# Loading the first batch ahead of the weights, and what shares memory with the set-up

## The chip, the cores and the metric

One core of one Trainium2 chip. The metric is the device time of one execution of the whole kernel in microseconds, the median over several runs. The profile is one further execution under the hardware profiler; it gives a span, from the first to the last instruction, and every instruction's place in it.

## The reference

32 graphs (batches b) of 512 nodes with 256 features. Two layers; each adds a graph attention and then a sequence model to x:

```python
# layer 0
x = x + gnn0(layernorm(x), adj, W, a_src, a_dst, ...)   # 4 heads, masked softmax over neighbours
x = x + mamba2(layernorm(x), W_in, conv_w, ..., W_lin)  # 512 channels, chunked scan over the nodes
# layer 1
x = x + gnn1(layernorm(x), adj, W, a)                   # one head
x = x + lstm(layernorm(x), W_ih, W_hh, ...)             # over the 512 nodes, with prefix and suffix sums
```

All in float32; adj is int32, 1 MB for each graph, and x 0.5 MB for each graph.

## The kernel before

The kernel runs two phases. `layers_per_batch` does layer 0 and the attention of layer 1 for each batch and writes the result to a buffer `X3` in device memory. `recurrence` then runs the LSTM of all 32 batches together, node by node. Between the two, a flag `odd` is read, and if it is set a general version of the first phase runs; with these inputs it isn't set.

**The set-up.** `layers_per_batch` first loads some 22 weights through the SP queue (`load_k` L96 for matrices, `load_row` L101 for rows spread over all partitions), in the order in which the code names them. Weights that only the set-up reads (`w0t`, `asrc`, `adst`, `normw`, `woutt`, `wlin`, `w1t`, `a1`) lie in a pool `wset`. From them TensorE (PE) makes the score weights of layer 0 (`pwa` L154, put into `sw0` by VectorE (DVE) at L205), of layer 1 (`pwb` L166, into `sw1` at L212) and the product `wc` of the output weights (`pwc` L243, L247). Then `wset` is closed, and the pools `io` (x and adj), `one`, `two` are opened over the same memory, so that a tile in them can be written only when the readers of what lay there are done.

**The batches.** `plain0(b)` loads adj (L474) and x (L476), normalises x (`layernorm` L65 to L71; its reciprocal root is two operations on GpSimd (POOL), `ve` L54 and `rs` L56), makes the mask and counts it (`msk` L481, `sqa` L483), turns x (`pxT` L262, `xT` L265), multiplies with `sw0` (`pra` L428), sends a row `linea` to device memory (L435) and has it spread over the partitions (`rb` L448), turns the mask (`pm` L493), projects (`phn` L507) and forms the weighted sum (`w` L461 and L467, `pav` L533). `after0` normalises the heads and adds to x (L319 to L337, POOL among them: L336, L337). `mamba_in` and `mamba_dt` prepare, `mamba` does the scan: `zs` L680, products of channels with decays read back through `ce` (L658) and `bc` (L736), POOL multiplications at L729, L776 and L800, and the output product `po` L830. `plain1` and `after1` do layer 1's attention and store to `X3`.

**The order.** Each part is a generator that yields between steps. `streams` holds one generator for each kind of work with a due time for each step, counted in batches; the step with the lowest due time is issued next:

```python
streams = [
    each((0.0, 1.0, mamba, 0)),
    each((-0.097, -0.026, mamba_in, 0), (-0.026, 0.192, mamba_dt, 0)),
    each((0.571, 0.86, second, -1), (0.86, 1.54, first, 2)),
    each((1.65, 1.76, after0, 2)),
]
```

From this order and its own costs of instructions a planner fixes at build time the order of every engine and of the SP queue; an instruction that is ready by its costs may come ahead of one that was issued earlier. On the chip each engine and queue follows its order and waits on semaphores.

**The recurrence's weights.** `recurrence_weights` (called rw here) is one more stream: it loads small pieces of the LSTM's weights (`rwl` L1061, `rwraw` L1097 and L1101), scales and reorders them on POOL (`ordered`: `rwt` L1050, L1054, L1105) and stores them to a buffer `wr` (L1089, L1109), which `recurrence` reads. Its due times run from 3.25 to about 25 batches. The first piece is issued while the streams are started, ahead of everything else.

Of the kernel before, what the change touches and what calls it, by code (L numbers as in the profile page):

```python
# [9 lines left out]
F32 = mybir.dt.float32  # L10
I32 = mybir.dt.int32
# [64 lines left out]
def layers_per_batch(ctx, tc, c, a, X3, odd=None, wr=None):  # L76
# [6 lines left out]
    nc = tc.nc  # L83
    nb = a.x.shape[0]
# [9 lines left out]
    def load_k(src, cols, name, pool=None):  # L94
        t = (pool or wp).tile([P, src.shape[0] // P, cols], F32, name=name)
        nc.sync.dma_start(out=t, in_=src.rearrange("(k p) c -> p k c", p=P))  # L96
        return t

    def load_row(src, name):
        t = wp.tile([P, src.shape[1]], F32, name=name)  # L100
        nc.sync.dma_start(out=t, in_=src.to_broadcast([P, src.shape[1]]))  # L101
        return t


    tri = wp.tile([P, P], F32, name="tri")
    late = wp.tile([P, P], F32, name="late")
# [14 lines left out]

    setup = ExitStack()
    wset = setup.enter_context(tc.tile_pool(name="wset", bufs=1))
    w0 = load_k(a.w0, D, "w0")
    w0t = load_k(a.w0t, D, "w0t", wset)
    asrc = load_k(a.asrc, T0, "asrc", wset)
    adst = load_k(a.adst, T0, "adst", wset)
    bias0 = load_row(a.bias0, "bias0")
    gamma = load_row(a.gamma, "gamma")
    beta = load_row(a.beta, "beta")  # L130
    win = load_k(a.win, DIN, "win")
    convw = load_k(a.convw, 4, "convw")
    convb = load_k(a.convb, 1, "convb")
    dtb = wp.tile([NH, 1], F32, name="dtb")
    nc.sync.dma_start(out=dtb, in_=a.dtb.rearrange("o h -> h o"))
    alog = load_row(a.alog, "alog")
    dcol = load_k(a.dcol, 1, "dcol")
    normw = load_k(a.normw, 1, "normw", wset)
    woutt = load_k(a.woutt, DI, "woutt", wset)
    wlin = load_k(a.wlin, D, "wlin", wset)  # L140
    blin = load_row(a.blin, "blin")
    w1 = load_k(a.w1, D, "w1")
    w1t = load_k(a.w1t, D, "w1t", wset)
    a1 = load_k(a.a1, 2, "a1", wset)

    def score_weights0(vec, half, name):

# [99 lines left out]
        nc.vector.tensor_scalar(wc[:, cc, :], pw[:, :D], normw[:, cc, :], None, ALU.mult)  # L247

    setup.close()
    io = ctx.enter_context(tc.tile_pool(name="io", bufs=2))  # L250
    one = ctx.enter_context(tc.tile_pool(name="one", bufs=1))
    two = ctx.enter_context(tc.tile_pool(name="two", bufs=2))

# [86 lines left out]
    def attention0(b, state):  # L340


        adj = io.tile([P, NT, N], I32, tag="adj", bufs=1, name=f"adj{b}")
        nc.sync.dma_start(out=adj, in_=a.adj[b].rearrange("(i p) j -> p i j", p=P))
        x = io.tile([P, NT, D], F32, tag="x", bufs=4, name=f"x{b}")
        nc.sync.dma_start(out=x, in_=a.x[b].rearrange("(i p) d -> p i d", p=P))
        xn = two.tile([P, NT, D], F32, tag="rowa", name=f"xn{b}")
        layernorm(nc, small, c, xn, x, NT)
        nc.gpsimd.tensor_tensor(x, x, beta.unsqueeze(1).to_broadcast([P, NT, D]), ALU.add)
# [120 lines left out]
    def plain0(b, state):  # L470


        adj = io.tile([P, NT, N], I32, tag="adj", bufs=1, name=f"adj{b}")
        nc.sync.dma_start(out=adj, in_=a.adj[b].rearrange("(i p) j -> p i j", p=P))  # L474
        x = io.tile([P, NT, D], F32, tag="x", bufs=4, name=f"x{b}")
        nc.sync.dma_start(out=x, in_=a.x[b].rearrange("(i p) d -> p i d", p=P))  # L476
        xn = two.tile([P, NT, D], F32, tag="rowa", name=f"xn{b}")
        layernorm(nc, small, c, xn, x, NT)
        nc.gpsimd.tensor_tensor(x, x, beta.unsqueeze(1).to_broadcast([P, NT, D]), ALU.add)
# [43 lines left out]
        for q in range(2):  # L523
# [3 lines left out]
            for m in range(NT // 2):  # L527
                w = weighted(rb, cols, 2 * q, m, adjT, f"{b}_{q}")
                yield
                for t in range(2):  # L530
                    j = 2 * m + t
# [5 lines left out]
                for t in range(2):  # L537
                    j = 2 * m + t
# [54 lines left out]
    def mamba_dt(b, state):  # L593

        mT = state["mT"]

        csr = one.tile([P, N], F32, tag="csr", name=f"csr{b}")
        dtr = csr[64 : 64 + NH, :]
        pd = bank(f"pdt{b}")
        for k in range(DK):  # L600
# [12 lines left out]
        raw = columns(dtr, c.ident[64 : 64 + NH, 64 : 64 + NH], f"raw{b}")  # L613
# [12 lines left out]
        q = small.tile([P, NT, NH], F32, tag="q", name=f"q{b}")  # L626
# [26 lines left out]
        nc.scalar.activation(dec.rearrange("p a i h -> p (a i h)"), pdc[:, : 2 * NT * NH], AF.Exp)  # L653
        yield

        ce = one.tile([P, NC, N - P], F32, tag="ce", name=f"ce{b}")
        for k in range(2):
            nc.sync.dma_start(  # L658
                out=ce[k * DS : (k + 1) * DS],
# [5 lines left out]
    def mamba(b, state):  # L665
        x, mT = state["x"], state["mT"]
# [16 lines left out]
        bT = one.tile([DS, N], F32, tag="bT", name=f"bT{b}")  # L683
        cT = one.tile([P, N], F32, tag="cT", name=f"cT{b}")
# [153 lines left out]
        ssr = one.tile([P, N], F32, tag="ssr", name=f"ssr{b}")  # L838
        nc.scalar.copy(ssr, pss)
        pst = bank(f"psc{b}")  # L840
        for i in range(NT):
# [121 lines left out]
    states = [{} for _ in range(nb)]  # L963
# [29 lines left out]
    ]  # L993
    if odd is not None:
        rw = ctx.enter_context(tc.tile_pool(name="rw0", bufs=1))
        streams.append(3.25 + (nb - 8) / 64 * n for n, _ in enumerate(recurrence_weights(nc, rw, a, wr)))
    END = nb + 10
    at = [next(t) for t in streams]
    while min(at) < END:
# [27 lines left out]
        nc.vector.tensor_scalar(odd, pf[:1, :1], P - 0.5, None, ALU.is_lt)  # L1027


def recurrence_weights(nc, pool, a, wr):  # L1030

# [13 lines left out]
    def tile_(p, n, tag):  # L1045
        return pool.tile([p, n], F32, tag=tag, name=tag)

    def ordered(raw, n, s):
# [5 lines left out]
            nc.gpsimd.tensor_scalar(halves[:, :, to, :], src, half[g] * s, None, ALU.mult)  # L1054
        return t


    wl = tile_(P, 2 * DK, "rwl")
    for q in range(Q):
        for l in range(2):  # L1060
            nc.sync.dma_start(  # L1061
# [2 lines left out]
            )  # L1064
    yield
    nc.gpsimd.tensor_tensor(wl[:, :DK], wl[:, DK:], wl[:, :DK], ALU.subtract)
    bl = tile_(P, 2, "rbl")
    nc.sync.dma_start(out=bl, in_=a.bl.to_broadcast([P, 2]))
    b = [tile_(P, 4 * J, f"rwraw{n}") for n in range(2)]
    for t, src in zip(b, (a.bih, a.bhh)):  # L1070
        nc.sync.dma_start(out=t[:Q], in_=src.rearrange("o (q r) -> (o q) r", q=Q))
    yield
# [7 lines left out]
    nc.sync.dma_start(out=wr[0][:, n0 + 2 * J : n0 + 2 * J + 8], in_=wr[1].rearrange("o (u p) -> p (o u)", p=P))  # L1080
    yield
    for n, src in enumerate((a.fw, a.bw)):
        t = tile_(P, W, "rwt")
        for q in range(Q):
            nc.sync.dma_start(out=t[q * GB : (q + 1) * GB, :J], in_=src[q : q + 1, :].to_broadcast([GB, J]))
        yield
        nc.gpsimd.tensor_scalar(t[:, :J], t[:, :J], 0.5, None, ALU.mult)
        yield
        nc.sync.dma_start(out=wr[0][:, n0 + n * J : n0 + (n + 1) * J], in_=t[:, :J])  # L1089
        yield  # L1090
    for n, (src, s) in enumerate(((a.wih, 1.0), (a.whh, 0.5))):
        for k in range(DK):
            for q in range(Q):
                raw = tile_(P, 4 * J, f"rwraw{q % 2}")
                cols = slice(q * 4 * J, (q + 1) * 4 * J)
                if n == 0:
                    nc.sync.dma_start(out=raw, in_=src[k * P : (k + 1) * P, cols])  # L1097
                else:
                    for r in range(Q):
                        r0 = r * J + k * 32  # L1100
                        nc.sync.dma_start(out=raw[r * 32 : (r + 1) * 32], in_=src[r0 : r0 + 32, cols])  # L1101
                yield
                t = ordered(raw, P, s)
                if n == 1:
                    nc.gpsimd.tensor_scalar(t[:, 4 * J : 4 * J + 1], wl[:, k : k + 1], 0.5, None, ALU.mult)  # L1105
                yield
                w = (4 * J, W)[n]
                o0 = n * nx + (k * Q + q) * w
                nc.sync.dma_start(out=wr[0][:, o0 : o0 + w], in_=t[:, :w])  # L1109
                yield  # L1110
# [361 lines left out]
```

## Time and profile before

| what | us |
|---|---|
| median of 3 runs (lowest, highest) | 4805.4 (4803.51, 4810.24) |
| the profiled execution | 4803.97 |
| its span | 4802.2 |
| busy in the span: PE / PE weight loads / DVE | 4177.1 / 2586.4 / 3438.4 |
| busy in the span: ScalarE (ACT) / POOL | 3084.4 / 1308.3 |
| first adj load leaves; last set-up product `wc` | 30.01; 29.50 |
| first `zs` of batch 0, 1, 31 | 129.1, 227.1, 3259.7 |
| first instruction of `recurrence` on DVE | 3369.95 |

In lines of the profile the columns are: start and duration in us, engine (SPq and ACTq are the queues that issue DMAs), source line, operation, tile written <- tiles read, shape, count, and in brackets the idle time of the engine just before, with what ended it. In a table by windows each engine's busy time stands with its number of instructions, then the granted PE clock as a share of full speed, the share of time in which the DMA engines were busy, and GB/s.

### The profile page before, as it was taken

How to read it: one execution, taken by the hardware profiler on the slowest of the kernel's cores; microseconds unless marked ns; L12 is line 12 of the kernel's file. 1: busy time of each engine (PE TensorE's matmuls, PEld its weight loads, DVE VectorE, ACT ScalarE, POOL GpSimd, SP SyncE). 2: the span in 40 equal slices, each digit the busy share in tenths (PEclk: the TensorE clock that was granted, in tenths of full speed). 3: DMA queues.
4: the chain of work that ended last, by engine and by line, in shares of the span. 5: the costliest groups of instructions: out<-in, count | busy, mean ns of one | idle time of the engine just before them, and what ended most of it. 6: DMA issues, size and time to landing. Idle time of an engine off the chain costs nothing. (4 is left out here: it accounts for less than half of the span.)

```text
span 4802.2 us, 105289 instructions
## 1 busy us (share of the span) xinstructions
PE 4177.1 (87%) x40654; PEld 2586.4 (54%) x40654; DVE 3438.4 (72%) x10207; ACT 3084.4 (64%) x6724; POOL 1308.3 (27%) x1012
## 2 busy tenths in 40 slices
PE   4888888888888888888888888887899999999993
PEld 2444454444444444444445444444677777777772
DVE  3566666677666666666666667664688888888887
ACT  3677667776777767677766777765455555555552
POOL 4333343333433334333334333341000000000000
PEclk7999999999999999999999999998999999999997
DMA  4221112211122111222112221111211111111115
GB/s 110 65 67 59 56 67 67 69 58 60 62 71 69 58 60 56 68 69 67 58 56 65 68 69 58 60 40 38 56 38 43 41 41 39 39 42 38 42 38 160
DMA packets 273672, 286.96 MB, mean 60 GB/s; under 512 B 152844, under 2 KB 224488, under 8 KB 270984
## 3 DMA queue, kind: packets, MB, share of 16 engines
q1 hardware_dynamic: 269784, 270.26, 19.1%
q10 hardware_dynamic: 3216, 9.81, 0.7%
q8 instruction: 324, 5.31, 0.5%
q14 instruction: 188, 1.54, 0.1%
q0 software_dynamic: 160, 0.04, 0.0%
HBM read 226.04 MB, written 37.11 MB: 55 GB/s over the span
## 5 line engine op out<-in xcount | busy, mean ns | idle before, releaser
L1263 PE MATMUL pg<-wall,h 128*32 128x128 f32 x16352 | 559.1, 276 | 13.6 <-DVE h L1340 10.3
L1240 PE MATMUL pu<-xTr,wall 128*128 128x256 f32 x2048 | 565.3, 399 | 0.0
L1263 PEld LDWEIGHTS pg<-wall,h 128*32 128x32 f32 x16352 | 419.2, 109 | 210.1 <-DVE h L1340 170.1
L467 DVE SCALAR_TENSOR_TENSOR w<-w,adjT 128x1024 f32<-128x1024 f32 x256 | 348.0, 1380 | 245.6 <-ACT w L461 245.6
L1323 ACT ACTIVATE z<-pg 128x128 f32<-128x128 f32 x1024 | 255.8, 278 | 249.6 <-PE pg L1263 248.6
L743 ACT ACTIVATE g<-bc,cs 128x128 f32<-128x128 f32 x1024 | 321.9, 391 | 137.8 <-PE py L811 137.8
L1240 PEld LDWEIGHTS pu<-xTr,wall 128*128 128x128 f32 x2048 | 348.7, 190 | 104.0 <-issue 76.4
L693 DVE SCALAR_TENSOR_TENSOR acc<-px,convw,acc 128x511 f32<-128x511 f32 (+2 forms) x480 | 347.2, 745 | 76.7 <-ACT acc L688 68.6
L1332 ACT ACTIVATE tc<-z 128x32 f32<-128x32 f32 x1024 | 234.4, 229 | 250.6 <-DVE z L1328 181.7
L461 ACT ACTIVATE w<-rb,neg,colsa 128x512 f32<-128x512 f32 x512 | 387.4, 806 | 11.8 <-DMA rb<-linea 7.4
L533 PE MATMUL pav<-w,hb 128*64 128x512 f32 x1024 | 351.2, 612 | 22.8 <-DVE w L467 22.8
L830 PE MATMUL po<-wc,xh 128*128 128x256 f32 x1024 | 283.5, 422 | 100.3 <-POOL xh L800 100.3
L729 POOL TENSOR_TENSOR ce<-ce,cT 128x384 f32<-128x384 f32 x128 | 185.2, 1477 | 665.2 <-ACT cT L701 648.0
L54 POOL TENSOR_SCALAR ve<-mv 128x4 f32<-128x4 f32 x32 | 6.2, 195 | 1292.0 <-DVE mv L1165 1292.0
L945 PE MATMUL pov<-wb,wv 128*128 128x257 f32 x1024 | 243.2, 390 | 90.8 <-DVE wv L467 90.8
L1252 PE MATMUL pg<-turner,xu 128*32 128x128 f32 (+1 forms) x8192 | 321.5, 273 | 0.0
L672 PE MATMUL px<-mT,win 128*128 128x512 f32 x640 | 306.8, 610 | 0.0
L1241 ACT ACTIVATE xu<-pu,wall 128x256 f32<-128x256 f32 x512 | 243.2, 475 | 89.1 <-PE pu L1240 74.8
L1327 DVE SCALAR_TENSOR_TENSOR ab<-z 128x64 f32<-128x64 f32 x1024 | 226.4, 221 | 83.0 <-ACT z L1323 57.0
L830 PEld LDWEIGHTS po<-wc,xh 128*128 128x128 f32 x1024 | 203.2, 213 | 145.5 <-POOL xh L800 116.2
L945 PEld LDWEIGHTS pov<-wb,wv 128*128 128x128 f32 x1024 | 191.4, 192 | 134.8 <-DVE wv L467 105.7
L56 POOL TENSOR_TENSOR rs<-ve,mhalf 128x4 f32<-128x4 f32 (+1 forms) x192 | 255.2, 1329 | 15.9
(244 smaller groups left out, 8865.6 us busy)
## 6 DMA issues: line engine op xcount, KB each, us to landing
bc<-line SPq DMA_DIRECT2D x128, 512.0 KB
adj<-in_adj_dram SPq DMA_DIRECT2D x32, 1024.0 KB
rb<-linea SPq DMA_DIRECT2D x64, 512.0 KB
ce<-line SPq DMA_DIRECT2D x64, 384.0 KB
x<-in_x_dram SPq DMA_DIRECT2D x32, 512.0 KB
X<-x SPq DMA_DIRECT2D x32, 512.0 KB
xt<-X SPq DMA_DIRECT2D x128, 128.0 KB
x<-X SPq DMA_DIRECT2D x128, 128.0 KB
```

Of the source, the lines that this page charges most:

```text
L461: nc.scalar.activation(w[:, t, k, :], rb[:, k, :], AF.Relu, bias=neg1, scale=cols[:, 2 * m + t, h + k : h + k + 1],)
L467: nc.vector.scalar_tensor_tensor(w[:, :, k, :], w[:, :, k, :], 1.0, edges, ALU.add, ALU.mult)
L533: nc.tensor.matmul(pa[k * HO : (k + 1) * HO, :], hb[:, j, 2 * q + k, :], w[:, t, k, :], start=(j == 0), stop=(j == NT - 1),)
L672: nc.tensor.matmul(pz, win[:, k, col : col + P], mT[:, k, :], start=(k == 0), stop=(k == DK - 1))
L693: nc.vector.scalar_tensor_tensor(acc[:, s:], pz[:, : N - s], convw[:, cc, k : k + 1], acc[:, s:], ALU.mult, ALU.add)
L743: nc.scalar.activation(g[:, i, k, :], bc[:, k, i * P : (i + 1) * P], AF.Relu, bias=cs[:, i, 2 * cc + k : 2 * cc + k + 1], scale=-1.0,)
L830: nc.tensor.matmul(po[:, i * D : (i + 1) * D], xh[:, cc, it * P : (it + 1) * P], wc[:, cc, :], start=(cc == 0), stop=(cc == NC - 1),)
L945: nc.tensor.matmul(po[:, : D + 1], ws[j // 2][:, j % 2, 0, it * P : (it + 1) * P], wb[:, j, :], start=(j == 0), stop=(j == NT - 1),)
L1240: nc.tensor.matmul(pu, wih[:, k, u, :], xT[:, k, :], start=(k == 0), stop=(k == DK - 1))
L1252: nc.tensor.matmul(p[q * GB : (q + 1) * GB, :], xu[:, 2 * q + n, r : r + GB], turner[:, : e - s], start=True, stop=(t == 0),)
L1263: nc.tensor.matmul(p[q * GB : (q + 1) * GB, :], h[k], whh[:, k, q, s:e], start=(start and k == 0), stop=(k == DK - 1))
L1323: nc.scalar.activation(z[n][:, H:], pgs[n][:, : 4 * H], AF.Tanh)
```

## The change

- `io` is opened at the start, beside the set-up's memory and no longer over it. The x of batch 0 is the first load on the SP queue, and its adj comes after layer 0's weights. `attention0` and `plain0` take these two for b = 0.
- The other weights are loaded in a new order: layer 0's first, then the rows, mamba's, w1 with its group, and the output weights last.
- `csr`, `ce`, `bT`, `cT` and `ssr` of mamba (one buffer each) move from `one` to a new pool `mam`, which is opened first over the memory of `wset`.
- `recurrence_weights` starts with a bare `yield`, so that its first piece is issued at its due time, 3.25. Every tile that it loads is first touched on POOL: `begun` copies one column (two for `rwl`) out of the x of the batch that is current at that due time, and the load has to wait for the copy.
- The due times of the streams are unchanged.

```diff
+    io = ctx.enter_context(tc.tile_pool(name="io", bufs=2))
+
+    def load_x(b):
+        x = io.tile([P, NT, D], F32, tag="x", bufs=4, name=f"x{b}")
+        nc.sync.dma_start(out=x, in_=a.x[b].rearrange("(i p) d -> p i d", p=P))
+        return x
+
+    def load_adj(b):
+        adj = io.tile([P, NT, N], I32, tag="adj", bufs=1, name=f"adj{b}")
+        nc.sync.dma_start(out=adj, in_=a.adj[b].rearrange("(i p) j -> p i j", p=P))
+        return adj
+
+    x0 = load_x(0)
...
-    w0 = load_k(a.w0, D, "w0")
     w0t = load_k(a.w0t, D, "w0t", wset)
     asrc = load_k(a.asrc, T0, "asrc", wset)
     adst = load_k(a.adst, T0, "adst", wset)
+    w0 = load_k(a.w0, D, "w0")
+    adj0 = load_adj(0)
+    beta = load_row(a.beta, "beta")
     bias0 = load_row(a.bias0, "bias0")
     gamma = load_row(a.gamma, "gamma")
-    beta = load_row(a.beta, "beta")
+    alog = load_row(a.alog, "alog")
+    blin = load_row(a.blin, "blin")
     win = load_k(a.win, DIN, "win")
...
-    alog = load_row(a.alog, "alog")
     dcol = load_k(a.dcol, 1, "dcol")
+    w1t = load_k(a.w1t, D, "w1t", wset)
+    a1 = load_k(a.a1, 2, "a1", wset)
+    w1 = load_k(a.w1, D, "w1")
     normw = load_k(a.normw, 1, "normw", wset)
     woutt = load_k(a.woutt, DI, "woutt", wset)
     wlin = load_k(a.wlin, D, "wlin", wset)
-    blin = load_row(a.blin, "blin")
-    w1 = load_k(a.w1, D, "w1")
-    w1t = load_k(a.w1t, D, "w1t", wset)
-    a1 = load_k(a.a1, 2, "a1", wset)
...
     setup.close()
-    io = ctx.enter_context(tc.tile_pool(name="io", bufs=2))
+    mam = ctx.enter_context(tc.tile_pool(name="mam", bufs=1))
...
     def plain0(b, state):
-        adj = io.tile([P, NT, N], I32, tag="adj", bufs=1, name=f"adj{b}")
-        nc.sync.dma_start(out=adj, in_=a.adj[b].rearrange("(i p) j -> p i j", p=P))
-        x = io.tile([P, NT, D], F32, tag="x", bufs=4, name=f"x{b}")
-        nc.sync.dma_start(out=x, in_=a.x[b].rearrange("(i p) d -> p i d", p=P))
+        x, adj = (load_x(b), load_adj(b)) if b else (x0, adj0)
...
-        streams.append(3.25 + (nb - 8) / 64 * n for n, _ in enumerate(recurrence_weights(nc, rw, a, wr)))
+        now = lambda: states[int(min(at))]["x"][:, 0, 0:1]
+        streams.append(3.25 + (nb - 8) / 64 * n for n, _ in enumerate(recurrence_weights(nc, rw, a, wr, now)))
...
-def recurrence_weights(nc, pool, a, wr):
+def recurrence_weights(nc, pool, a, wr, now):
...
+    def begun(t, *columns):
+        for n in columns or (0,):
+            nc.gpsimd.tensor_copy(t[:, n : n + 1], now())
+        return t
+
+    yield
+
-    wl = tile_(P, 2 * DK, "rwl")
+    wl = begun(tile_(P, 2 * DK, "rwl"), 0, DK)
...
-    bl = tile_(P, 2, "rbl")
+    bl = begun(tile_(P, 2, "rbl"))
...
-    b = [tile_(P, 4 * J, f"rwraw{n}") for n in range(2)]
+    b = [begun(tile_(P, 4 * J, f"rwraw{n}")) for n in range(2)]
...
-        t = tile_(P, W, "rwt")
+        t = begun(tile_(P, W, "rwt"))
...
-                raw = tile_(P, 4 * J, f"rwraw{q % 2}")
+                raw = begun(tile_(P, 4 * J, f"rwraw{q % 2}"))
```

More of the change, by code (lines that the diff above doesn't have):

```diff
@@ L470, in plain0 @@
     def plain0(b, state):
[L473 to L476, printed above, removed]
+        x, adj = (load_x(b), load_adj(b)) if b else (x0, adj0)
         xn = two.tile([P, NT, D], F32, tag="rowa", name=f"xn{b}")
@@ L595, in mamba_dt @@
         mT = state["mT"]
-        csr = one.tile([P, N], F32, tag="csr", name=f"csr{b}")
+        csr = mam.tile([P, N], F32, tag="csr", name=f"csr{b}")
         dtr = csr[64 : 64 + NH, :]
@@ L654, in mamba_dt @@
         yield
-        ce = one.tile([P, NC, N - P], F32, tag="ce", name=f"ce{b}")
+        ce = mam.tile([P, NC, N - P], F32, tag="ce", name=f"ce{b}")
         for k in range(2):
@@ L682, in mamba @@
         xh = two.tile([P, NC, N], F32, tag="wide", bufs=4 if odd is not None else 3, name=f"xh{b}")
-        bT = one.tile([DS, N], F32, tag="bT", name=f"bT{b}")
-        cT = one.tile([P, N], F32, tag="cT", name=f"cT{b}")
+        bT = mam.tile([DS, N], F32, tag="bT", name=f"bT{b}")
+        cT = mam.tile([P, N], F32, tag="cT", name=f"cT{b}")
         def convolved(cc):
@@ L837, in mamba @@
             nc.tensor.matmul(pss[32 * cc : 32 * (cc + 1), :], ones[:, :32], zs[:, cc, :], start=True, stop=True)
-        ssr = one.tile([P, N], F32, tag="ssr", name=f"ssr{b}")
+        ssr = mam.tile([P, N], F32, tag="ssr", name=f"ssr{b}")
         nc.scalar.copy(ssr, pss)
```

## The prediction

> **What bounds the kernel now.** I read the busy time by stage first, then the order of time in the first 130 us, then the waits of the SP queue, and last two neighbouring batches of the long middle part. The stage table (start:end, length, then busy us of PE, PEld, DVE, ACT, POOL, the granted PE clock, the DMA share, GB/s):
>
> ```profile
> 0.00:35.70 35.70, 12.02 (x56) 10.61 (x56) 7.86 (x60) 1.49 (x2) 5.40 (x21) 0.99 0.62 144
> 35.70:129.10 93.40, 54.16 (x212) 25.58 (x212) 40.20 (x86) 37.68 (x60) 48.08 (x90) 0.73 0.35 102
> 1341.00:2352.00 1011.00, 871.46 (x4283) 482.15 (x4282) 678.82 (x1321) 719.72 (x1257) 386.46 (x260) 0.98 0.20 63
> 3380.00:4802.20 1422.20, 1341.17 (x26858) 1014.71 (x26858) 1240.97 (x5861) 765.48 (x2686) 39.97 (x67) 0.98 0.20 50
> ```
>
> The set-up (to 35.7) and the first batch alone (to 129.1) leave every engine mostly idle: 129 us in which latency decides. From 129.1 to 3264, 31 batches pass at about 101 us each, with PE busy 86 to 88%. The recurrence takes the rest; the change has no instruction in it. In order of time, around the end of the set-up (start, duration, engine, line, what, and the idle time before with its releaser):
>
> ```profile
> 17.68 4.75 SPq L1061 DMA_DIRECT2D rwl<-in_wl_dram  x8
> 21.89 1.78 PEld L166 LDWEIGHTS pwb<-a,w1t 128*128 128x128 f32 x8 [12.79 <-issue]
> 23.62 5.84 PE L243 MATMUL pwc<-wlin,woutt 128*128 128x256 f32 x16
> 29.50 0.48 DVE L247 TENSOR_SCALAR wc<-pwc,normw 128x256 f32<-128x256 f32 x1 [0.38 <-PE pwc L243]
> 30.01 0.38 SPq L474 DMA_DIRECT2D adj<-in_adj_dram  x1
> 35.72 2.00 ACT L483 ACTIVATE sqa<-adj,neghalf 128x2048 bf16<-128x2048 int32 x1 [20.10 <-DMA adj<-in_adj_dram]
> 37.18 0.75 DVE L65 BATCH_NORM_STATS2 bnst<-x 128x6 f32<-128x256 f32 x2 [0.22 <-DMA x<-in_x_dram]
> 40.57 2.08 ACT L71 ACTIVATE xn<-x,off,rs 128x256 f32<-128x256 f32 x4 [2.75 <-DVE off L69]
> ```
>
> The load of the first adj leaves at 30.01, right after the last `wc` (29.50 + 0.48), because its buffer lies over the set-up's `wset`. It lands at 35.72, x at 37.18. Nothing of batch 0 runs before. Further on, still batch 0:
>
> ```profile
> 93.11 1.36 POOL L1054 TENSOR_SCALAR rwt<-rwraw 128x64 f32<-128x64 f32 x4
> 94.55 0.21 POOL L54 TENSOR_SCALAR ve<-vs 128x16 f32<-128x16 f32 x1
> 103.59 0.71 POOL L1054 TENSOR_SCALAR rwt<-rwraw 128x64 f32<-128x64 f32 x2
> 104.25 2.34 POOL L337 TENSOR_TENSOR x<-x,o 128x1024 f32<-128x1024 f32 x1
> 122.22 0.87 SPq L448 DMA_DIRECT2D rb<-linea  x2
> 126.95 0.81 ACT L461 ACTIVATE w<-rb,neg,colsa 128x512 f32<-128x512 f32 x1 [6.01 <-DMA rb<-linea]
> ```
>
> The recurrence's weights (rw: L1054, L1109, all of them between 17.68 and 140 us) stand in POOL's way and, worse, in SP's. The SP queue's own waits of the first 150 us:
>
> ```profile
> SPq L1109 <- POOL rwt L1054: 26.4, 8, 6.6
> SPq L1109 <- POOL rwt L1105: 25.2, 7, 10.7
> ```
>
> So SP sat 51.6 us in the stores of rw. The row `linea` of batch 1 was sent at 112.37, its `rb` left only at 122.22.
>
> [...] its clock records hold half-clock stretches of 3.41 us, two in every two batches while a batch takes 100.7, two in every batch while it takes 102.2. [...] `o` L335 takes 3.35 us against a median of 1.225 where POOL's 2.34 us `x` L479 starts 0.07 us before it. [...]
>
> **Part 1: x and adj of batch 0 first, in memory of their own.** From 30.01 to 35.72 the 1 MB of adj took 5.71 us; the 0.5 MB of x behind it took another 1.46. That gives 2.92 us for 1 MB and 2.8 fixed. Afterwards x leaves at 0.79 and should land at 0.79 + 2.8 + 1.46 = **5.1** (before 37.18). Then come w0t, w0 (0.25 MB each) and adj: 2 MB in all, so adj lands near 0.79 + 2.8 + 5.8 = **9.4** (before 35.72). The score weights `sw0` were ready at 10.0 and slip by the 0.4 us issue and 1.46 us of x in front: 11.5. From x landed to xT took 43.21 + 1.07 - 37.18 = 7.1 us, so xT would be there at 12.2[...]. `pra` L428 began at 43.94; it begins at 12.5 to 15.5, **-28 to -31**. I take -29. adj has 5 us to spare before `pm` L493.
>
> **Part 2: what loses its cover.** `pwb` (1.84 us of PE) and `pwc` (5.84), with 14 + 4 DVE operations (3 us), ran before batch 0; now they fall into its chain. SP needs 16.9 us for the 22 weights, and two loads stand in front; wlin, the last, lands near 20 to 23. Batch 0 wants PE for `pm` and `phn` (7.5 us) from about 19. If the fixed order of PE has `pwc` ahead of them, all wait; if it falls where PE waits for `w` L467, it is free. Bounds 0 and +14 (7.7 of work, 6 of waiting); I take +4. alog and beta go forward, the w1 group goes ahead of woutt: needed late, 0.
>
> **Part 3: rw leaves the first batches.** On the chain of batch 0: `ve` began at 94.55, its input was there at 91.69: 2.9. `x` L337: 104.25 against 103.58: 0.7. Its layernorm afterwards (109.05 to 110.07, 110.26 to 111.0): 1.7. Sum 5.3. The late `rb` held ACT for 6.0 just ahead of mamba's `zs` at 129.1, but the following batch took only 98.1 against 100.5, so 2.6 is made up already; 3 stays. Together **-8**, bounds 0 and -11.
>
> **Part 4: rw in batches 3 to 25.** The median durations of its rows (68 x 0.37, 17 x 0.10, 8 x 0.22, the rest) sum to about 32 us of POOL; `begun` adds 23 copies of one column, not in the trace; by the nearest row, L1105, 0.22 each: 5 us. POOL is 38.7 of 100.5 us busy, so most hides in its idle stretches of 21 and 15 us. But POOL is on PE's path in after0, about 1500 to 1518 of its batch (18%):
>
> ```profile
> 1511.40 2.51 POOL L800 TENSOR_TENSOR xh<-xh,zs 128x512 f32<-128x512 f32 x2
> 1516.55 1.69 POOL L800 TENSOR_TENSOR xh<-xh,zs 128x512 f32<-128x512 f32 x1 [1.26 <-DVE xh L799]
> ```
>
> PE waits 3.2 us there. 18% of 37 us is +6.6; bounds 0 and +37. `begun` makes each load wait for POOL, and the SP queue behind it: `bc`, `ce`, `rb` can be late by what POOL is late. SP has only ten DMAs in a batch, with two buffers of `bc`; I take 0 and keep +10. The stretch of two neighbouring speeds:
>
> ```profile
> 1739.30:1839.80 100.50, 86.54 (x431) 47.63 (x430) 68.02 (x134) 72.23 (x126) 38.76 (x26) 0.98 0.20 64
> 1941.00:2043.20 102.20, 88.25 (x431) 48.92 (x430) 68.00 (x135) 72.21 (x127) 38.71 (x26) 0.97 0.20 63
> ```
>
> Same instructions, 1.7 us more PE time: one more half-clock window of 3.4 us. Batches 5 and 18 to 21 are slow so, 9 us in all. PE gaps moved by rw can change which batches hit a window: -9 to +28 (22 batches x 1.7 less the 9). I take +4.
>
> **Part 5: `mam`.** csr, ce, bT, cT and ssr must wait for the readers of `wset`; csr is first written at 118.77 and would be at some 80, 45 us after the last `wc`. Nothing.
>
> **Sum.** -29 + 4 - 8 + 6.6 + 4 = **-22** us. The profiled execution took 4803.97 (span 4802.2), 1.4 below the median of 4805.4; so 4782 to 4783, and I say **4782**. A measurement of this kernel can tell about 0.2% from no change: 9.6 us, that is below 4796 or above 4815.
>
> **Rivals.**
> 1. *Late weights* (15%). The in-order engines stop at `pwb`/`pwc` or `sw1` until the last load lands, and batch 0 starts behind them all the same. For it: PE, DVE and ACT each run one fixed order. Against it: 20 us of other work is ready. Part 2 becomes +14, the change -12: 4793.
> 2. *The clock takes it back* (11%). Most batches fall into the two-window rhythm: +28 in place of +4, so 4806, no difference. For it: the kernel drops into that rhythm by itself. Against it: it also leaves it by itself.
> 3. *rw on the path of PE* (12%), the slower side. Each of the 16 blocks (`begun`, load, five POOL operations of 1.9 us, store) lands in the stretch where PE waits for POOL, and the longer gap costs a half-clock window too: 16 x (1.9 + 1.7) = 58 in place of 10.6, so 4829. It decides from about 12 of the 16. Against it: that stretch is 18% of a batch.
> 4. *The change doesn't do what it says* (2%): batch 0 still waits, for `sw0` or beta, past 30 us: 4805.
>
> My forecast keeps 60%, 4768 to 4795. Faster by over 0.2%: 0.60 with rival 1's 0.15, 0.75; within 0.2%: 0.13; slower: 0.12. The range reaches down to the sum of the best ends of parts 1 to 3 and of the clock, -2 - 4 - 3 - 13 from the forecast, 4760, and up to rival 2 with half of what rival 1 adds, 4806 + 5 = 4811; rival 3 and part 4's worst end stay outside.
>
> **What would show it.** Right: first LN on DVE by 6 us, `pra` by 16, first `zs` at 95 to 100 in place of 129.1, no rw load before 380 us, batches at 100.5 to 102.5. Wrong: `pm` held behind `pwc` (part 2); `zs` early but batches 3 to 25 above 102.5 (part 4), with longer idle time of PE before `po` L830; first `bnst` after 20 us (rival 4). If the first `zs` is 30 us early and the total is not, the middle took it.

## The result: no difference, and the profile after

| what, us | before | after |
|---|---|---|
| median of 12 runs (lowest, highest) | 4802.74 (4800.05, 4810.24) | 4803.34 (4797.82, 4812.22) |
| the profiled execution | 4803.97 | 4809.66 |
| first `zs` of batch 0 | 129.1 | 97.2 |
| from there to the first `zs` of batch 31 | 3130.7 | 3165.5 |
| from there to the end of the span | 1542.4 | 1545.2 |
| half-clock windows of PE in the 31 batches | 45 | 65 |

The ratio after to before is 1.0004, 95% interval 0.9995 to 1.0012. The profiled execution of after lies 6.3 us above its median, so its parts are compared with the profiled execution of before: 31.9 us gained in the head, 34.8 lost in the middle, 2.8 lost at the end. Some 5 us of this loss belong to this one execution, since before's lies only 1.2 above its median. The windows are the stretches of 3.41 us in the clock records of the trace in which the granted clock is 0.5.

The table by windows of after (its third row is the whole middle):

```profile
0.00:35.70 35.70, 21.26 (x104) 15.71 (x104) 14.36 (x87) 12.69 (x21) 8.63 (x19) 0.95 0.82 241
35.70:97.20 61.50, 38.23 (x140) 12.90 (x141) 29.39 (x49) 25.91 (x40) 17.18 (x11) 0.75 0.11 39
97.20:3262.70 3165.50, 2725.56 (x13205) 1508.79 (x13203) 2096.13 (x4091) 2225.34 (x3881) 1237.63 (x921) 0.96 0.20 62
3380.00:4807.00 1427.00, 1343.91 (x26864) 1016.09 (x26864) 1243.31 (x5870) 766.28 (x2688) 41.19 (x69) 0.97 0.20 51
```

In the first 35.7 us every engine does about half as much again as before, or more, and DMA moves 241 GB/s in place of 144. The recurrence is as it was. The head in order of time:

```profile
4.87 0.75 DVE L65 BATCH_NORM_STATS2 bnst<-x 128x6 f32<-128x256 f32 x2 [3.77 <-DMA x<-in_x_dram]
9.80 1.28 ACT L494 ACT_TABLE_LOAD   x1 [9.80 <-DMA adj<-in_adj_dram]
11.09 2.00 ACT L494 ACTIVATE sqa<-adj,neghalf 128x2048 bf16<-128x2048 int32 x1
13.94 0.21 ACT L252 ACTIVATE aneg<-alog 128x8 f32<-128x8 f32 x1 [0.75 <-DMA alog<-in_alog_dram]
14.05 2.06 ACT L71 ACTIVATE xn<-x,off,rs 128x256 f32<-128x256 f32 x4
17.36 3.59 PE L442 MATMUL pra<-xT,sw 128*48 128x512 f32 x4 [0.51 <-issue]
20.89 1.05 PE L182 MATMUL pwb<-a,w1t 128*128 128x2 f32 x8
26.37 4.24 PE L259 MATMUL pwc<-wlin,woutt 128*128 128x256 f32 x16
30.45 2.75 PE L518 MATMUL phn<-w,xT 128*128 128x256 f32 x12
```

x is there at 4.87 and adj at 9.80. ACT keeps its order and has `sqa`, which waits for adj, and `aneg`, which waits for alog, ahead of `xn`: the last input of `xn`, `off`, was there at 11.44, `xn` starts at 14.05, and so `pra` at 17.36. `pwc` stands in the middle of `phn`.

The middle is where it went. On POOL in order of time, around the end of a batch: two neighbouring batches of before, 9 and 10, then batch 9 of after.

```profile
1116.62 2.90 POOL L588 TENSOR_TENSOR x<-x,blin 128x1024 f32<-128x1024 f32 x1 [1.13 <-ACT xm L71]
1120.39 2.43 POOL L479 TENSOR_TENSOR x<-x,beta 128x1024 f32<-128x1024 f32 x1 [0.87 <-ACT xn L71]
1126.81 0.19 POOL L54 TENSOR_SCALAR ve<-ssc 128x4 f32<-128x4 f32 x1 [3.99 <-DVE ssc L844]
...
1227.32 0.19 POOL L54 TENSOR_SCALAR ve<-ssc 128x4 f32<-128x4 f32 x1 [2.27 <-DVE ssc L844]
```

```profile
1095.62 2.91 POOL L599 TENSOR_TENSOR x<-x,blin 128x1024 f32<-128x1024 f32 x1 [1.14 <-ACT xm L71]
1098.59 1.06 POOL L1071 COPY rwraw<-x 128x1 f32<-128x1 f32 x1
1102.03 1.36 POOL L1066 TENSOR_SCALAR rwt<-rwraw 128x64 f32<-128x64 f32 x4 [2.37 <-DMA rwraw<-in_wih_dram]
1103.35 2.35 POOL L490 TENSOR_TENSOR x<-x,beta 128x1024 f32<-128x1024 f32 x1
1105.64 0.10 POOL L1062 MEMSET rwt<- 128x2 f32 x1
1105.83 0.19 POOL L54 TENSOR_SCALAR ve<-ssc 128x4 f32<-128x4 f32 x1
```

Before, POOL waited for `ssc` ahead of `ve`: 3.99 us in a batch with a half-clock window at `po`, which makes `ssc` late, and 2.27 in one without; so throughout its batches 1 to 28 (in batch 20 it was 4.27). In after the copy of `begun` waits for x of L599, the load waits for the copy, `rwt` waits 2.37 us for the load to land, and POOL, in order, holds `x` L490 and `ve` behind it. That is 1.06 + 2.37 + 1.36 = 4.8 us, of which 0.9 fall into a wait that was there ahead of L490: 3.9 in all. It fits into 3.99 and not into 2.27. The other 15 pieces stand at the same place of their batches (6 to 23). In batches 8, 9, 10, 22 and 23 `ve` started 1.07 to 1.88 us after its `ssc`, in 6, 7, 13, 14 and 18 by 0.16 to 0.66, in all batches of before by 0.09. That is 10 us in all; the rest of the loss shows as windows.

### The profile page after: what moved, and what is told of

It is laid out like the page before. It is cut to its first block, busy times and chain, and to the rows that moved or that the text cites. A ratio compares the mean times of both kernels' runs of the same rounds, so it can differ in the third digit from the quotient of the medians.

```text
span 4807.9 us, 105303 instructions
## 1 busy us (share of the span) xinstructions
PE 4204.3 (87%) x40654; PEld 2601.4 (54%) x40654; DVE 3436.7 (71%) x10207; ACT 3085.3 (64%) x6724; POOL 1320.9 (27%) x1035
## 5 line engine op out<-in xcount | busy, mean ns | idle before, releaser
L841 PE MATMUL po<-wc,xh 128*128 128x256 f32 x1024 | 290.6, 431 | 96.4 <-POOL xh L811 96.4
L841 PEld LDWEIGHTS po<-wc,xh 128*128 128x128 f32 x1024 | 208.6, 218 | 143.4 <-POOL xh L811 110.5
```

The lines of the kernel that those rows point to most:

```text
L841: nc.tensor.matmul(po[:, i * D : (i + 1) * D], xh[:, cc, it * P : (it + 1) * P], wc[:, cc, :], start=(cc == 0), stop=(cc == NC - 1),)
```

## The experiments

The times are medians of 4 runs or more, in brackets the ratio to the kernel before run beside them, with its 95% interval. That kernel lay at 4798.2 to 4803.2, so a difference between two groups of runs is uncertain by some 5 us. Windows, first `zs` and the middle (from the first `zs` of batch 0 to that of batch 31) are of the profiled execution. The fast rhythm is the one of before: 100.7 us a batch on average and one half-clock window; the slow one has 102.2 to 102.4 us and two. My first theory: the head's gain is real, and rw in the middle throws the batches into the rhythm of two half-clock windows. The rival: something else in the change (`mam`, order, buffers) slows the batches.

**1. The changed kernel with rw as it was before** (no bare `yield`, no copies):

```diff
-            nc.gpsimd.tensor_copy(t[:, n : n + 1], now())
+            pass
...
-    yield
```

> The changed kernel with rw as it was before: no bare yield at its start, begun copies nothing; the new loads, their order and mam stay. Theory (rw's perturbations in batches 3 to 25 hold the middle in the rhythm of two half-clock windows in a batch, and that took the head's gain): first zs 5 to 10 us later than in the changed kernel (102 to 107), 31 to 42 half-clock windows in the 31 batches, total 4770 to 4782. Rival (the new memory or the earlier start itself puts the middle into the slow rhythm, rw has no part in it): 60 windows or more, total 4800 to 4812.

4771.95, ratio 0.995 (0.9937 to 0.9964); first `zs` 102.0, 41 windows, middle 3125.0. The rest of the change gains 27 us in the head, 26 in the median, and the batches keep the fast rhythm.

**2. The kernel before with rw's part alone** (`yield`, `begun`, `now`):

> The kernel before with rw's part of the change alone: bare yield, begun, due times that hold. Theory: the head gains 5 to 10, the middle goes to 55 to 70 half-clock windows and loses 20 to 40: total 4815 to 4835. Rival (rw has no part in the loss): 4793 to 4799.

4817.01, 1.0042 (1.0028 to 1.0055); first `zs` 114.8, 59 windows, middle 3157.3. rw's part gains 14.3 us in the old head and loses 26.6 in the middle: by itself it makes the kernel slower. The rival falls with these two. By the traces PE, DVE and ACT run the same instructions in the same order in both of them, in before and in after (from the first `zs` of batch 1 to that of batch 30): where they differ, it is on POOL and in the SP queue.

Two neighbouring batches of experiment 1, then one of after:

```profile
708.30:809.10 100.80, 87.07 (x430) 48.44 (x430) 68.00 (x135) 72.18 (x127) 38.69 (x26) 0.98 0.20 63
809.10:909.60 100.50, 87.93 (x431) 48.88 (x430) 68.16 (x135) 72.27 (x127) 38.72 (x26) 0.97 0.21 64
```

```profile
701.40:803.80 102.40, 88.34 (x431) 48.89 (x430) 68.09 (x135) 72.28 (x127) 41.09 (x32) 0.97 0.20 64
```

**3. rw packed closer**, over batches 3 to 7 (`(nb - 8) / 384` in place of `(nb - 8) / 64`) in the changed kernel:

> The changed kernel with rw's due times six times as dense: from 3.25 to about 7 batches in place of 3.25 to 25; begun stays, the work is the same. Theory (rw costs next to nothing itself, but each of its small delays can throw the batches back into the two-window rhythm): slow or uneven until batch 7 or 8, then the one-window rhythm as in the kernel before; 38 to 50 half-clock windows in the 31 batches; total 4772 to 4788. Rival (the same rw work costs the same wherever it stands): 4800 to 4810.

4782.67, 0.9967 (0.9954 to 0.9979); first `zs` 98.2, 48 windows. Batches 3 and 4 took 105.5 and 108.5, and from batch 10 on the fast rhythm is back, but for batches 14, 15 and 29. The middle, 3141.3, loses 16 us against experiment 1, where after loses 41: most of the loss goes with the number of batches that carry rw.

**4. Useless products to keep PE busy.** In the full-clock windows right ahead of a half-clock one, batches 1 to 29, the longest wait of PE stood mostly at two places: at the product `pst` (L794, for `xdd`) in 17 of 34 in before and 25 of 52 in after, at `po` (L841, for `xh`) in 17 and 22. My guess was that work for PE in these waits would save the windows. Seven kernels tried it. The first edit goes ahead of each `pst`, the second ahead of all of `po`, the third, into a bank of its own, right ahead of the product of `po` that waits:

```diff
+            nc.tensor.matmul(pst, bn[:, i].rearrange("p two n -> p (two n)"), xdt[:, i, :], start=True, stop=True)
...
+            for n in range(3 if j == 0 else 0):
+                nc.tensor.matmul(po, ones, g[:, :2].rearrange("p i k l -> p (i k l)"), start=True, stop=True)
...
+                    for n in range(3 if it == 0 and cc == NC - 1 else 0):
+                        nc.tensor.matmul(idle, ones, g[:, :2].rearrange("p i k l -> p (i k l)"), start=True, stop=True)
```

(a) The first two together, in the changed kernel and in the kernel before:

> The changed kernel, and PE does work without use where it waits for POOL: before each of the three pst products the same product with xdt, before po three products of ones with g, 0.85 us each; the real products overwrite them. Theory: [...] the windows of the middle nearly all go (under 15 in 31 batches), batches take about 99 us, total 4695 to 4720. Rival (the clock is only a sign, the batches are late for waits on rw): batches stay near 102, total 4795 to 4815.

> The kernel before with the same PE work without use. Theory: under 15 half-clock windows in the 31 batches, total 4730 to 4755, and the changed kernel with this work is 25 to 35 us faster than this one (the head's gain, once the clock takes none of it). Rival (rw in the middle costs by itself what the head gains): the two within 10 us of each other.

4847.29 (1.0102, 1.0086 to 1.0117) and 4866.45 (1.0140, 1.0124 to 1.0155), 60 and 62 windows: missed. The windows moved to other places. But both have the same rhythm now, and between them the changed kernel is 19 us ahead, less than the 25 to 35 expected.

(b) The second alone, with two products in place of three, in the changed kernel, in that of experiment 1, and in the kernel before:

> The changed kernel with two products without use (ones with g, 0.85 us each) ahead of po alone, where PE waits for POOL; rw stays in the middle. The order of PE, DVE, ACT and POOL is nearly that of the changed kernel this time. Theory (the loss is the second half-clock window, at po): no window is left there, at most one in a batch, at pst; batches at 99 to 100.9; 25 to 40 windows; total 4750 to 4775. Rival (the clock is only a sign): total 4798 to 4812.

> Head edits with rw early, and the two products ahead of po. Theory: both gains: 15 to 31 windows in the 31 batches, total 4740 to 4765. Rival (one window in a batch is the least, whichever place gives it): as rw early alone, 4768 to 4778.

> The kernel before with the two products ahead of po. Theory: its middle has some 38 windows, half of them at po; without those 15 to 31 stay, total 4768 to 4788, and the changed kernel with the same products is 10 to 30 us faster, since the head's gain is no longer taken. Rival: 4797 to 4806.

4821.01 (1.0042, 1.0029 to 1.0055), 4814.5 (1.0034, 1.0022 to 1.0046), 4840.75 (1.0083, 1.007 to 1.0096); 62, 60 and 56 windows: missed. Why, a batch of the second shows (PE in order of time):

```profile
588.18 1.88 PE L839 MATMUL po<-g,ones 128*128 128x512 f32 x4
589.90 1.46 PE L843 MATMUL po<-wc,xh 128*128 128x256 f32 x6
593.28 4.54 PE L843 MATMUL po<-wc,xh 128*128 128x256 f32 x12 [1.92 <-POOL xh L811]
```

The useless products run as soon as they can, the real ones behind them, and the wait is still there, 1.92 us. Batches 1 to 9 of this kernel took 102.4 us each, and all 31 on average 102.2 (3166.8 in all), although it has no rw in the middle.

(c) The third alone, in the changed kernel and in that of experiment 1:

> The changed kernel, rw in the middle. Three products without use (0.85 us each, into a bank of their own) stand right where PE waits 3.2 us for the last xh: after the first three products of po, before the fourth; in the runs before this one they stood ahead of all of po and the wait behind them stayed 1.9 us. Theory (the loss is the second half-clock window in a batch, at po): no window at po, 25 to 38 in the 31 batches, total 4752 to 4785. Rival (po's window is not what takes the time, or another place takes its part): over 55 windows or total over 4798.

> Head edits with rw early (4772 without the products), and the three products at the wait in po. Theory: only pst can still trigger the half clock, 15 to 32 windows, total 4745 to 4772. Rival (the place shifts and the kernel locks on to two windows elsewhere): 4795 to 4815.

4864.63 (1.013, 1.011 to 1.015), 64 windows, and 4844.51 (1.0093, 1.0075 to 1.011), 49 windows: missed. The window at `po` went; useless work of some 2 us in each batch and windows elsewhere came.

**5. The wait itself made shorter.** The last of the four products `xh`*`zs` of a batch goes to DVE, so that `po` no longer waits for POOL's third and fourth product one after the other:

```diff
-            nc.gpsimd.tensor_tensor(y, y, zs[:, cc, :], ALU.mult)
+            (nc.vector if cc == NC - 1 else nc.gpsimd).tensor_tensor(y, y, zs[:, cc, :], ALU.mult)
```

In the kernel of experiment 1, in the changed kernel, and in the kernel before:

> Head edits with rw early; the last of the four products of xh with zs goes to DVE in place of POOL, so that po's wait gets shorter by about 1 us without work for PE. If the wait at po is what sets both the batch's length and its half-clock window: batches of 98 to 99.5, 15 to 32 windows, total 4715 to 4760. Rival (DVE has no time to spare there, or its order shifts): 4768 to 4800.

> The changed kernel with the last of each batch's four xh*zs products on DVE in place of POOL, so that `po` no longer waits for POOL's third and fourth product one after the other. rw stays in batches 3 to 25. With rw early the same edit gave 4741 and 29 windows in 31 batches. Theory (rw's own delays cost nearly nothing, the second window does, and that window hangs on po's wait): 4740 to 4760, under 40 windows. Rival (rw in the middle costs some 30 us wherever the windows fall): 4765 to 4785, about 48 or more windows.

> The kernel before with the last xh*zs product on DVE, nothing else. It differs from the fastest kernel so far (4741, first zs 102.0, 29 windows) by the head alone: x and adj first, new load order, mam. Theory (the head's gain of 27 us is untouched by what the middle does): first zs about 129, some 29 windows, 4762 to 4772. Rival (a later start shifts the batches against the windows and changes their number): outside of that by more than 8 us, with the number of windows to match.

4740.83 (0.9876, 0.9857 to 0.9895), 29 windows, middle 3090.9; 4788.85 (0.9973, 0.9963 to 0.9982), 48 windows, middle 3148.0; 4760.93 (0.9914, 0.9901 to 0.9927), 43 windows, middle 3101.2. The first was confirmed: most batches take 98.9 and have no window. PE's wait at `po`, in after and then in the first of these three:

```profile
784.12 2.15 PE L841 MATMUL po<-wc,xh 128*128 128x256 f32 x7 [3.20 <-POOL xh L811]
```

```profile
1680.24 3.72 PE L841 MATMUL po<-wc,xh 128*128 128x256 f32 x16 [2.24 <-DVE xh L811]
```

The second was not confirmed: it ended by the rival, and 4 us beyond it. With the faster batches rw costs 48 us (46 by the kernel before beside each), not nearly nothing. The third lies 1 us below what was expected, 20 above the first and not 27, and with 14 more windows than the first. The trace of the second shows rw at work in the open (POOL, DVE, ACT, PE):

```profile
1499.81 1.06 POOL L1071 COPY rwraw<-x 128x1 f32<-128x1 f32 x1
1504.09 1.36 POOL L1066 TENSOR_SCALAR rwt<-rwraw 128x64 f32<-128x64 f32 x4 [3.22 <-DMA rwraw<-in_wih_dram]
1507.91 0.19 POOL L54 TENSOR_SCALAR ve<-ssc 128x4 f32<-128x4 f32 x1
1509.26 0.48 DVE L859 SCALAR_TENSOR_TENSOR x<-po,rs,x 128x256 f32<-128x256 f32 x1 [4.31 <-POOL rs L56]
1511.06 0.68 ACT L447 ACTIVATE rowsa<-pra,mxa 12x512 f32<-12x512 f32 x1 [3.62 <-DVE mxa L445]
1511.79 0.41 PE L452 MATMUL pca<-ident,rowsa 8*128 8x8 f32 x4 [2.91 <-ACT rowsa L447]
```

`rwt` waits 3.22 us for its load, `ve` stands behind it, and `rs`, x, `rowsa` and PE follow one after the other, until PE waits 2.91 us. In the first of the three, without rw in the middle, PE has no wait at this product:

```profile
1693.90 0.28 PE L452 MATMUL pca<-ident,rowsa 8*128 8x8 f32 x2
```

In the second `ve` was late by more than 0.1 us in 17 batches (the expectation of experiment 7 says 18), 34.0 us in sum. So my theory that rw "costs nearly nothing itself" fell; a new one was that POOL standing behind the landing of the load is rw's cost.

**6. rw's two sides apart**, each as a stand-in on top of experiment 1, from batch 7.4 on, 16 times. POOL alone: a memset, the copy of x, and `rwt`'s memset and four scalings, with no DMA. DMAs alone: copy, pinned load, store. Both, with `rwt`'s work on columns that the load doesn't write. And the wait: copy, pinned load, one scaling of what it brought, store. The edit of the wait, shortened; the comments say where the other three differ:

```diff
+    streams.append(7.375 + (nb - 8) / 64 * n for n, _ in enumerate(stand_in(nc, rw, way, a, now)))
...
+                nc.gpsimd.tensor_copy(raw[:, 0:1], now())
+                nc.sync.dma_start(out=raw, in_=src[k * P : (k + 1) * P, cols])       # not with POOL alone
+                yield
+                nc.gpsimd.tensor_scalar(t, raw[:, :J], 0.5, None, ALU.mult)          # the wait; POOL alone and both: x4, not of the load
+                yield
+                nc.sync.dma_start(out=dump[:, :J], in_=t)
```

> rw early as in the first experiment (4772, 41 windows), plus a stand-in for rw's POOL work alone: from 7.375 batches on, once for each of the 16 pieces, the copy of one column of the current x and the memsets and four scalings of rwt on tiles of its own, no DMA. If POOL's small delays are what drops the kernel into two windows: 4790 to 4810, 55 or more windows. If SP's waits do it: 4770 to 4780, about 41 to 45 windows.

> rw early as in the first experiment (4772, 41 windows), plus a stand-in for rw's DMAs alone: 16 loads, each pinned behind the copy of one column of the current x on POOL, and 16 stores; of POOL's work only those 16 copies of some 0.2 us. If SP's waits (late rb, late bc) are what drops the kernel into two windows: 4790 to 4810, 55 or more windows. If POOL's work does it: 4770 to 4780, about 41 to 45 windows. If both this and the POOL-only kernel stay low, it takes the two together.

> rw early (4772, 41 windows) plus both stand-ins in one, uncoupled: 16 times from batch 7.4 on, a pinned load, a store, and five POOL operations of rwt's size on columns that the load doesn't write, so that POOL never waits for the load to land. If the two small delays only have to add up to drop the kernel into two windows: 4790 to 4815, 55 or more windows. If it takes what both stand-ins lacked, POOL standing in order behind the landing of the pinned load (38 us in all in the changed kernel): 4772 to 4783, about 41 to 46 windows.

> rw early plus the pinned loads with a single short POOL operation (one scaling of 64 columns) that reads what the load brings, and a store of it: POOL's wait for the landing, some 2.4 us for each of 16, without rwt's other work. If that wait is what drops the kernel into two windows: 4790 to 4810, 55 or more windows. If it is the sum of POOL's work and SP's waits: 4772 to 4783, about 41 to 46 windows.

4778.19 (0.9951, 0.9938 to 0.9964) with 44 windows, 4778.24 (0.9953, 0.9941 to 0.9966) with 44, 4787.19 (0.9972, 0.9962 to 0.9983) with 49, and 4797.3 (0.9985, 0.9977 to 0.9992) with 55. Against experiment 1 POOL's work and SP's pinned loads cost 6 us each, both together 15, between its two expectations. The wait, with a quarter of `rwt`'s work, costs 25, as its first expectation had it. But experiment 1 belongs to another group of runs. By the kernel before beside each, the four cost 3, 3, 12 and 22, so that the cost of the first two is hardly clear of noise. The groups of POOL's scalings between 400 and 3000 us, in the kernel with POOL alone and in that with the wait (busy us, mean ns, idle us before them and what ended it):

```profile
L1061 POOL TENSOR_SCALAR st<-sraw 128x64 f32<-128x64 f32 x64 | 21.9, 372 | 1.4
```

```profile
L1061 POOL TENSOR_SCALAR st<-sraw 128x64 f32<-128x64 f32 x16 | 6.0, 375 | 40.5 <-DMA sraw<-in_wih_dram 20.6 <-DMA sraw<-in_whh_dram 19.9
```

POOL alone has 21.9 us of work and next to no idle time before it; the wait has 6.0 of work behind 40.5 of standing still. `ve` was late by more than 0.1 us in no batch of POOL alone or the DMAs alone, in one of both together, in four of the wait. POOL's work alone fits ahead of `ve`: where it stood in a batch of the fast rhythm, 0.43 to 0.45 us of the 2.27 were left.

**7. rw moved behind `ve`.** The changed kernel with the DVE product (4788.85), and the copies taken from `zs` of the batch, which comes later than `ve`:

```diff
+        state["zs"] = zs
...
-        now = lambda: states[int(min(at))]["x"][:, 0, 0:1]
+        def now():
+            b = int(min(at))
+            return states[b if "zs" in states[b] else b - 1]["zs"][:, 0, 0:1]
```

> The changed kernel with the last xh*zs product on DVE (4789 so far), and rw's copies taken from zs of the batch instead of x, so that copy, load and rwt stand on POOL behind `ve<-ssc` and `rs`, ahead of a stretch of some 20 us in which POOL is idle, and no longer ahead of `ve<-ssc`; the order of PE, DVE and ACT is the same. In every kernel without rw in the middle `ve<-ssc` started 0.09 us after its `ssc`; in the kernel with 4789 it was up to 2.9 us late in 18 batches, 34 us in all. Theory (POOL standing behind rw's landing ahead of `ve<-ssc` is what rw costs): `ve<-ssc` at 0.09 again, under 36 windows, 4735 to 4755. Rival (rw's pinned loads or its work in the middle cost this wherever they stand): 4775 to 4795, 45 or more windows.

4735.2 (4716.33 to 4744.54), ratio 0.9841 (0.9824 to 0.9857): 53.7 us under the same kernel with rw ahead of `ve` (55.1 by the kernel before beside each), and 5.6 under the fastest so far (4740.83), whose runs its own overlap. On POOL:

```profile
1085.90 2.45 POOL L490 TENSOR_TENSOR x<-x,beta 128x1024 f32<-128x1024 f32 x1 [0.86 <-ACT xn L71]
1090.32 0.19 POOL L54 TENSOR_SCALAR ve<-ssc 128x4 f32<-128x4 f32 x1 [1.98 <-DVE ssc L856]
...
1101.16 0.18 POOL L1075 COPY rwraw<-zs 128x1 f32<-128x1 f32 x1
1104.73 3.29 POOL L1070 TENSOR_SCALAR rwt<-rwraw 128x64 f32<-128x64 f32 x4 [3.38 <-DMA rwraw<-in_wih_dram]
1110.26 0.10 POOL L1066 MEMSET rwt<- 128x2 f32 x1 [2.23 <-DMA wr<-rwt]
1122.23 2.94 POOL L741 TENSOR_TENSOR ce<-ce,cT 128x384 f32<-128x384 f32 x2 [11.87 <-ACT cT L713]
```

POOL still waits for the load, 3.38 us, but in a stretch with nothing close behind it: 11.87 us are left over ahead of `ce`. `ve` starts 0.09 us after `ssc` in all 32 batches. The number of windows was expected under 36 and is 43, the middle 3103.2 in place of 3148.0. Of these 44.8 us 34.0 are `ve`'s lateness, and five windows fewer make some 8: here most of the time came from `ve`, not from the clock. The order of PE, DVE and ACT is the same in the two traces. SP's queue was not relieved: between 400 and 3000 us it waited 163 us for POOL around the 16 pieces (loads and stores) with the copies from x, and 146 with those from `zs`.

## Why the prediction was wrong

It said 4782, faster; measured was 4803.34, no difference. Its own sentence for that case held: the first `zs` came 31.9 us earlier and the total did not, so the middle took it.

**Part 1** (-29) gave 43.94 - 17.36 = 26.6. x (5.1 forecast, 4.87), adj (9.4, 9.80) and `sw0` were as worked out. (For `sw0` 10.0 + 0.4 + 1.46 makes 11.9 and not 11.5; it was there at 11.37.) `pra` was 2 us later than the bound, because the sum took the chain of x alone and not ACT's order: ahead of `xn` stand `sqa` with its table load of 1.28, which wait for adj, and `aneg`, which waits another 0.75 for alog. The bound itself, 15.5, was an estimate; 2.4 of it are the 32 `sw` operations, as they were in before (0.16 + 0.28 + 0.36 + 1.64). So alog was not "needed late, 0", as part 2 has it.

**Part 2** (+4): from `pra` to `w` 15.1 us, before 13.6, so 1.5. `pwc` did stand inside `phn`: ACT waited 5.52 us for the first `phn` (`hn` at 31.94), with `w` right behind at 32.43. But `w` also needs `rb`, and its semaphore was complete only at 32.23, so hardly any of it was lost to `pwc`. `rb` left at 28.25, 4.7 us after `linea` at 23.57; in before it left 1.6 after it. From 23.5 to 28.3 the DMA engines were fully busy, at 367 to 390 GB/s, with what SP had issued up to 21.8 (the last weights, x and adj of the next batch), and `linea`, on ACT's queue, landed among it; in before they moved 14 GB/s between `linea` and `rb`. The prediction had no term for this, so that part 2 came out small is no confirmation of its sum. Rival 1 didn't happen.

**Part 3** (-8): from `w` to the first `zs` 64.8, before 71.6, so -6.8. The head in all: -31.9 against -33.

**Part 4** is the step that failed, in both of its terms. The total of +10.6 for the middle was +34.8.

- *The term for POOL's path, 18% of 37 us.* It spread rw evenly over the batch. But `begun` ties every copy to one x, and the planner puts the load's user right behind the load: each of the 16 pieces stands at the same place, ahead of `ve`. The trace of before had the price: POOL's slack there is 2.27 us in one batch and 3.99 in the next. And POOL's work by itself was not the cost, since it fits into 2.27. What doesn't fit is the wait for the landing on top of it, 2.37 us of 4.8, which the prediction looked for on SP ("can be late by what POOL is late") and not on POOL itself. `begun`'s copy was put at 0.22 and took 1.06.
- *The term for the clock, +4 with a bound of +28.* The trace of before had both rhythms, and I let most batches stay in the fast one. From batch 4 on most batches of after had two windows: 20 more at 1.7 us is 34. Rival 2, at 11%, named this end and 4806. But it let the kernel drop into the slow rhythm by itself, and without rw in the middle (experiment 1) it doesn't stay there: rw brings it.

How the two belong together: a batch of the fast rhythm that carries a piece of rw is 1.7 us late through `ve` (3.9 - 2.27 = 1.6), and a batch of the slow rhythm isn't, since its half-clock `po` makes `ssc` 1.7 us later anyway. Both are then 102.2 to 102.4 long. In after, batch 10 had one window and took 102.3; batch 6 had two and took 102.4. The kernel of experiment 2 shows it more often: six of its batches (7, 9, 13, 15, 16 and 22) had one window and a `ve` 1.58 to 1.89 us after `ssc`, and took 102.0 to 102.3. So while rw runs nothing faster than the slow rhythm is to be had with the copy at that place. That most of these batches show the window and not the late `ve` fits a batch of 102.4 us being 30 windows of 3.413, so that each batch meets the windows where the last one did; that this holds them there was not tested by itself. The middle follows the count of windows all the same, in the kernels without useless products and with POOL's product as it was:

| kernel | windows | middle, us | 3125.0 + 1.7 x (windows - 41) |
|---|---|---|---|
| rw early (1) | 41 | 3125.0 | 3125.0 |
| POOL alone, DMAs alone (6) | 44, 44 | 3130.2, 3128.7 | 3130.1 |
| before | 45 | 3130.7 | 3131.8 |
| rw packed (3) | 48 | 3141.3 | 3136.9 |
| both apart, the wait (6) | 49, 55 | 3137.7, 3148.0 | 3138.6, 3148.8 |
| before with rw's part (2) | 59 | 3157.3 | 3155.6 |
| after | 65 | 3165.5 | 3165.8 |

This is a fit and no proof that the windows are the cause: in experiment 2 the six batches above lost as much without a second window, so that its row meets the line in part by chance. The kernels with the DVE product don't lie on such a line (43 windows: 3101.2 and 3103.2; 48 windows: 3148.0). There `po`'s wait is 2.24 us in place of 3.20, POOL's slack ahead of `ve` is mostly 1.98, and rw's 34 us of late `ve` come in the open.

**Part 5** (nothing) and **rival 3**: nothing in the runs speaks against `mam` costing nothing. Rival 3's 58 us were for rw on PE's path at 16 places. It had the wrong stretch (`po`'s wait stayed 3.20 us). That rw costs 57 us of the middle with the DVE product (3148.0 - 3090.9) is near its 58 by luck: another kernel and another place.

Open: the changed kernel with the copies from `zs`, but with POOL's product as it was, wasn't run. So it is shown that the place ahead of `ve` is what rw costs with the DVE product. Without it, the stand-in with POOL's wait for the landing brings 14 of the 24 windows between experiment 1 and after, of which the pinned loads by themselves bring 3. The other 10 are not accounted for one by one. It is not shown that moving the copies would by itself bring the changed kernel back to 4772 or less. Nor is it known why the profiled execution of experiment 7, the slowest of its five at 4744.54, drops to two windows from about batch 22 on; the other four had a higher granted clock (0.971 to 0.977 against 0.969).

## What to carry to other kernels

Background work that is tied to an event lands at the same place of every batch: cost it against the slack of the in-order engine at that place, the wait for its own load included, and not by its busy time spread over the batch. Tie it to an event with an idle stretch behind it. And where the trace shows a loop in two rhythms of the clock, count the half-clock windows in every comparison; here 24 of them went with 41 of the 3125 us of the batches.

## What the runs showed of the hardware

- Half-clock windows came behind windows in which PE was busy for less than half of the time, and in none of these was it idle throughout. The clock records give the grid of windows of 3.413 us, and PE's records how long it was busy in each. In before and after, batches 1 to 29, PE was busy less than 0.41 of 57 full-clock windows, and a half-clock window followed every one of them. Of 84 with 0.41 to 0.5 it followed 29, and of 1495 with more than 0.5 none. The longest idle stretch in a full-clock window ahead of a half-clock one was 2.91 us. The ends of PE's products are modelled in the profile, so the shares are rough.
- The fast rhythm took 201.4 us for two batches, the length of 59 windows of 3.413; the slow one, where it was steady, 102.4 for one, the length of 30.
- One column copied on POOL took 1.06 to 1.07 us at the place after L599, in all 19 copies that after has there. Each of them ended 0.04 to 0.05 us behind a DVE operation on two inputs that had begun before it (`x` L872, 1096.34 to 1099.61; the copy 1098.59 to 1099.66). At the later place of experiment 7 a copy took 0.18. The prediction priced it at 0.22, by a row from another place.
- Useless products for PE never helped here: each of seven kernels with them was slower than the one without, by 18 to 73 us.
